# Joining a slot's score matmuls and V matmuls, and writing the mask with ScalarE, in a six-layer local-attention kernel

## The chip, the cores and the metric

The kernel runs on one core of a Trainium2 chip. The core has a matmul engine (TensorE, PE in the profile, with PEld for its weight loads), a vector engine (VectorE, DVE), an activation engine (ScalarE, ACT), a general engine (GpSimd, POOL) and a queue that issues DMAs (SyncE, SP). Each engine takes its own instructions in order; between engines they wait for semaphores. Matmul results go to PSUM, which has eight banks of 128 partitions by 512 fp32 numbers; everything else lives in SBUF. The metric is device time in microseconds; the profile is of one execution.

## The reference

The input `x` has shape (8, 512, 128): 8 sequences of 512 rows. Two residual blocks follow each other. The first is a layer norm, a linear recurrence with `tanh` over the 512 rows, and another layer norm. The second is a layer norm and six layers of local attention and a gated FFN:

```
def step(h, xb_t):
    h = jnp.tanh(h @ A.T + xb_t)
...
for i in range(DEPTH):
    x = attn_layer(shift_tokens(x), Wqkv[i], q_scale[i], k_scale[i], Wo[i]) + x
    x = ffn_layer(shift_tokens(x), ln_g[i], ln_b[i], W1[i], b1[i], W2[i], b2[i]) + x
```

Attention has 16 heads of 64. Queries and keys are normalised to length 1, scaled and rotated. A block of 32 queries sees 64 keys: its own 32 and the 32 before them. What lies outside the band of 32 back is masked, and so are the keys before the first row:

```
mask = (it < jb) | (it > jb + w) | (jb == -1)
sim = jnp.einsum('bhwie,bhwje->bhwij', bq, bk2) * QK_SCALE
sim = jnp.where(mask, -jnp.finfo(sim.dtype).max, sim)
attn = jax.nn.softmax(sim, -1)
out = jnp.einsum('bhwij,bhwje->bhwie', attn, bv2)
```

## The kernel before

The attention's work is cut into 96 groups, listed in `todo`. In layers 1 to 5 a group is one sequence and one half of the heads (8 heads: 4 pairs, `GP`). In layer 0, whose input comes out of the recurrence row by row, a group is 128 rows of four sequences and one half of the heads (`ChunkGroup`). A group is worked through in four slots, t = 0 to 3, of 128 queries each.

`slot(n, t)` writes out by hand, in program order, what the engines do in one slot. It works on several groups at once: the scores of group n at t (`cur`), the transposed probabilities and V products of the slot before (`last`, one slot late), the transposed outputs two slots late (`back`), the norms and values of group n+1 (`one`), and in slots 2 and 3 the query and key projections of group n+2 (`two`). Five lists `fill[0]` to `fill[4]` hold the work that stands between the pieces of attention; `run(k)` issues one of them. The engines take the instructions in this order.

The steps that the change and the prediction touch:

- `mask` (line 617): four bf16 matmuls of a 64x64 block of the identity with the mask array write the mask into two PSUM banks (`sc`, one per head of a pair) and open the accumulation.
- `scores` (line 634): small fp32 matmuls of 64 rows by 32 columns, which run beside each other in the array, add the scores. Each counts as two in the profile. A slot has 64 in the profile: 32 for pairs 0 and 1, 32 for pairs 2 and 3. The two halves are called apart, with `turn`, `turn_back` and `run(1)` between them.
- `less_max` (line 651): VectorE takes the maximum (L654) and subtracts it (L657); this frees the two banks.
- `exps` (line 663): ScalarE takes the exponential (L664). From group 9 on it stands before `run(2)`, in groups 0 to 8 behind it.
- `turn` (line 666): PE transposes the probabilities into `tp` (L670), ScalarE copies them out as `eT` (L675). `turn_back` (line 713) does the same for the outputs (`at` L718, `aoT` L722).
- `average` (line 677): the V products `av` (L689), again 32 and 32, in the two `acc` banks that `tp` and `at` had before. `divide` (line 699) is VectorE's reciprocal (L706) and product (L707), which frees those banks.
- `unit_a` and `unit_b` (lines 498, 512): projections `rawa` and `rawb` (L504, L516), ScalarE's squares (L508, L520) and scaled copy `bs` (L522), VectorE's `t` (L494), and GpSimd's two operations (L526, L527).
- `sums` (`nsq`, L533, copied as `ns`, L543), `norms` (`nt`, L415, then VectorE's solve, L427 to L437), `norms_back` (`kt`, L444, and ScalarE's copy `kn`, L451), `spread` (`bc`, L559), `finish` (VectorE's L567 and the DMAs of `qT` and `kbuf`), `values` (`vps`, L589, copied into `vbuf` by ScalarE, L598), `between` (DMAs inside `vbuf`), `project` (`yo`, L727) and `add` (L738).
- In the groups of layer 0 up to group 8 the recurrence runs inside the slots: `rec.tick(us)` (line 370) adds up the PE work issued, and issues one step (a matmul L295 and a `tanh` L303) when it reaches `PACE`, 0.35, and resets the sum. One call issues at most one step. `rec.need(c)` (line 377) issues what is missing of chunk c, steps and VectorE pieces, when a group needs it.
- `Feed` (line 816) is the FFN of four sequences. It takes part in the slots of 11 groups: in slot 0 `centre` stands in `fill[2]` and `fill[3]`, in slot 2 `apply` stands before `less_max`. The twelfth runs behind the last group.

PSUM is full: two banks for `sc`, two for `acc`, and four for all other products (`mm`; in the recurrence three and one for `xb`).

Of the kernel before, what the change touches and what calls it, by code (L numbers as in the profile page):

```python
# [7 lines left out]
F32 = mybir.dt.float32  # L8
# [6 lines left out]
B, S, D = 8, 512, 128  # L15
P = 128
DEPTH = 6
HEADS = 16
DH = 64
# [8 lines left out]
GP = 4  # L28
NG = NPAIR // GP

QB = 32
KB = QB + WINDOW
NT = S // P
# [15 lines left out]
def mk_seq_preln_kernel(  # L49
# [18 lines left out]
    nc = tc.nc  # L68
# [97 lines left out]
    with tc.tile_pool(name="qk", bufs=2) as qkp, tc.tile_pool(  # L166
        name="ao", bufs=1
    ) as aop, tc.tile_pool(name="tmp", bufs=2) as tmp, tc.tile_pool(
        name="e", bufs=1
    ) as ep, tc.tile_pool(name="small", bufs=4) as small, tc.tile_pool(  # L170
        name="rec", bufs=1
# [213 lines left out]
        rec = Recurrence()  # L385

        def shifted(b, buf):

            xs = xbufs[buf]
            nc.sync.dma_start(xs[: D // 2, WINDOW:], xT[: D // 2, b, :])  # L390
            nc.sync.dma_start(xs[D // 2 :, WINDOW + 1 :], xT[D // 2 :, b, : S - 1])
            return xs
# [61 lines left out]
        class Group:  # L454
# [161 lines left out]

            def mask(self, t):


                sct = scp.tile([P, 2, S], F32, tag="sc", name=f"sc_{self.nm}_{t}")  # L620
                self.sc = sct[:, :, : GP * KB].rearrange("p a (i k) -> p a i k", k=KB)
                for blk in range(2):
                    for par in range(2):
                        rows = slice(par * DH, (par + 1) * DH)
                        nc.tensor.matmul(
                            self.sc[blk * DH : (blk + 1) * DH, par],
                            ident_b[rows, rows],
                            mask_sb[rows, 0 if blk == 0 and self.first(t) else 1],
                            start=True,
                            stop=False,  # L630
                            skip_group_check=True,
                        )

            def scores(self, t, pairs):
                for i in pairs:
                    for blk in range(BT):
                        for par in range(2):
# [10 lines left out]
                            )  # L648
                rec.tick(0.4)

# [25 lines left out]

            def average(self, t, pairs):
                if pairs[0] == 0:
                    self.avs = [
                        accp.tile(  # L680
                            [P, GP, P], F32, tag="acc", name=f"av_{self.nm}_{t}_{par}"
                        )
                        for par in range(2)
                    ]
                for i in pairs:
                    for blk in range(BT):
                        for par, av in enumerate(self.avs):
# [8 lines left out]
                            )  # L696
                rec.tick(0.4)

# [296 lines left out]
        def slot(n, t, feed=None):  # L995
# [60 lines left out]
            if cur:  # L1056
                cur.mask(t)
                cur.scores(t, (0, 1))
            if last:
# [3 lines left out]
            run(1)  # L1063
            if cur:
                cur.scores(t, (2, 3))
            if feed and t == 2:
# [8 lines left out]
            if cur and n < NREC:  # L1075
                cur.exps()
            if last:
                last.average(lt, (0, 1))
            if one and t == 1:
                one.finish(1)  # L1080
                if not feed:
                    one.finish(2)
                    one.finish(3)
            run(3)
            if last:
                last.average(lt, (2, 3))
                last.divide(lt)
# [80 lines left out]
def _constants():  # L1168
# [4 lines left out]
    f = np.float32  # L1173
# [92 lines left out]
```

## Time and profile before

| | us |
|---|---|
| median of three runs | 4030.38 |
| lowest, highest | 4025.12, 4033.03 |
| span of the profiled execution | 4029.1 |
| PE busy | 3780.6 (94%) |
| DVE busy | 2496.4 (62%) |
| ACT busy | 1859.4 (46%) |
| POOL busy | 1824.5 (45%) |
| mask matmuls (L625, layers 1 to 5), busy | 97.1, 1280 matmuls |
| score matmuls (L641, layers 1 to 5), busy | 295.7, 20480 matmuls |
| V matmuls (L689, layers 1 to 5), busy | 307.6, 20480 matmuls |

The times agree within 0.2%, and the profiled execution lies 1.3 us under the median. Busy time is the time in which at least one instruction of the engine runs; matmuls are pipelined, so it is not time at PE's peak. In the profile's groups a row gives the line, the engine, the operation, output and inputs by the program's names, and then busy time, mean duration, and the idle time before it with what ended it. In a timeline a row begins with the start and the duration in microseconds; matmuls of one kind that follow each other stand in one row with their count, and a bracket holds the idle time of the engine just before and what ended it. The stride, from one row's start to the next one's on PE, tells what a piece costs, since PE's ends overlap.

### The profile page before, as it was taken

The page shows a single profiled execution, that of the slowest core. Times are in us where ns is not written, and L with a number is a line of the kernel's source. Part 1 is how long each engine was busy: PE and PEld are TensorE (multiplying, and loading weights), DVE is VectorE, ACT ScalarE, POOL GpSimd, SP SyncE. Part 2 cuts the span into 40 slices and gives each one's busy share as a digit, 9 for nine tenths or more (in the row PEclk, how much of TensorE's full clock was granted, in tenths as well). Part 3 has the DMA queues.
Part 4 walks back from the last instruction along what each step waited for, and adds up shares of the span by engine and source line. Part 5 has one row for each costly group of instructions (what it writes and reads, how often), then busy time and mean ns, then how long its engine had stood idle before and what let it go on. Part 6 is the DMA issues. An engine that isn't in the chain of part 4 may idle for free.

```text
span 4029.1 us, 147937 instructions
## 1 busy us (share of the span) xinstructions
PE 3780.6 (94%) x64726; PEld 1982.0 (49%) x64726; DVE 2496.4 (62%) x5209; ACT 1859.4 (46%) x3696; POOL 1824.5 (45%) x781
## 2 busy tenths in 40 slices
PE   5798997999999999999999999999999999999997
PEld 4555564444444444445444445454454444444453
DVE  3345646666576566566566566566566666676663
ACT  1243343445445455455455455455455445455442
POOL 0143323535355356366366366355355355355350
PEclk9888878999999999999999999999999999999998
DMA  3042343554344355344345345245344355354342
GB/s 108 23 109 64 87 96 75 117 128 93 84 110 110 72 116 117 83 111 111 73 107 127 79 102 119 65 112 129 74 104 113 69 123 120 75 113 106 74 108 61
DMA packets 366032, 389.51 MB, mean 97 GB/s; under 512 B 96974, under 2 KB 262348, under 8 KB 365260
## 3 DMA queue, kind: packets, MB, share of 16 engines
q1 hardware_dynamic: 364380, 378.09, 41.0%
q8 instruction: 512, 8.39, 0.9%
q10 hardware_dynamic: 1008, 1.96, 0.1%
q14 instruction: 132, 1.08, 0.1%
HBM read 34.25 MB, written 14.20 MB: 12 GB/s over the span
## 4 chain that ended last, share of the span: by engine, by line
PE 77%; DVE 13%; ACT 5%; issue 3%; DMA 1%; SPq 1%; ACTq 0%; DVEq 0%
PE vps L589 7%; PE yo L727 6%; PE rawb L516 6%; PE rawa L504 5%; PE sc L641 5%; PE tp L670 5%; PE xb L295 4%; PE av L689 4%; PE nsq L533 4%; PE at L718 4%; PE yf L948 3%; PE fa L922 3%; DVE t L567 3%; PE fg L926 3%; PE bc L559 2%
## 5 line engine op out<-in xcount | busy, mean ns | idle before, releaser
L526 POOL TENSOR_TENSOR u<-rope_sb,bs 128x1024 f32<-128x1024 f32 x320 | 766.4, 2395 | 1437.9 <-ACT bs L522 1311.1
L527 POOL TENSOR_TENSOR t<-t,u 128x1024 f32<-128x1024 f32 x320 | 755.7, 2362 | 25.1
L494 DVE SCALAR_TENSOR_TENSOR t<-rawa,par_sb,rope_sb 128x1024 f32<-128x1024 f32 x320 | 408.9, 1280 | 206.8 <-ACT sq L508 196.6
L664 ACT ACTIVATE e<-e 128x512 f32<-128x512 f32 x320 | 201.7, 630 | 609.6 <-DVE e L657 602.8
L567 DVE TENSOR_TENSOR t<-t,bc 128x1024 f32<-128x1024 f32 x320 | 376.5, 1215 | 159.0 <-PE bc L559 159.0
L689 PEld LDWEIGHTS av<-vbuf,eT 64*32 64x32 f32 x20480 | 208.4, 106 | 367.8 <-issue 254.0
L504 PE MATMUL rawa<-xbuf,wqk 128*128 128x512 f32 x640 | 357.7, 641 | 2.3 <-DMA xbuf<-xT 1.3
L589 PE MATMUL vps<-wv,xbuf 128*64 128x256 f32 x2560 | 346.7, 393 | 0.0
L516 PE MATMUL rawb<-xbuf,wqk 128*128 128x512 f32 x640 | 343.8, 619 | 0.0
L727 PE MATMUL yo<-aoT,wo 128*128 128x512 f32 x640 | 296.0, 605 | 41.4 <-DVE t L567 40.8
L641 PEld LDWEIGHTS sc<-kbuf,qT 64*32 64x32 f32 x20480 | 191.9, 106 | 245.2 <-issue 206.7
L689 PE MATMUL av<-vbuf,eT 64*32 64x65 f32 x20480 | 307.6, 224 | 3.0 <-issue 1.5
L508 ACT ACTIVATE sq<-rawa 128x512 f32<-128x512 f32 x320 | 188.3, 588 | 241.3 <-PE rawa L504 241.0
L295 PEld LDWEIGHTS xb<-hT,s1w 128*128 128x128 f32 x1022 | 202.8, 239 | 189.8 <-ACT hT L303 119.4
L641 PE MATMUL sc<-kbuf,qT 64*32 64x64 f32 x20480 | 295.7, 223 | 0.3 <-issue 0.3
L654 DVE TENSOR_REDUCE mx<-sc 128x8 f32<-128x512 f32 x320 | 220.0, 687 | 110.0 <-PE sc L641 110.0
L707 DVE TENSOR_TENSOR ao<-av,rc 128x256 f32<-128x256 f32 x640 | 271.8, 425 | 22.0
L675 ACT COPY eT<-tp 128x512 f32<-128x512 f32 x320 | 189.0, 591 | 188.2 <-PE tp L670 188.2
L295 PE MATMUL xb<-hT,s1w 128*128 128x8 f32 x1022 | 223.7, 292 | 44.1 <-ACT hT L303 43.3
L303 ACT ACTIVATE hT<-xb 128x8 f32<-128x8 f32 x512 | 91.0, 178 | 355.3 <-PE xb L295 338.0
L657 DVE TENSOR_TENSOR e<-sc,mx 128x512 f32<-128x512 f32 x320 | 221.3, 692 | 17.7 <-DVE mx L654 0.9
L670 PE MATMUL tp<-ident,e 128*128 128x128 f32 x1280 | 208.4, 285 | 18.6 <-DVE rc L706 15.8
(321 smaller groups left out, 6093.2 us busy)
## 6 DMA issues: line engine op xcount, KB each, us to landing
qT<-t SPq DMA_DIRECT2D x640, 128.0 KB
kbuf<-t SPq DMA_DIRECT2D x640, 128.0 KB
vbuf<-vbuf SPq DMA_DIRECT2D x544, 130.0 KB
vbuf<-vbuf SPq DMA_DIRECT2D x160, 97.5 KB
xbuf<-xT SPq DMA_DIRECT2D x95, 128.0 KB
xbuf<-xT SPq DMA_DIRECT2D x80, 127.8 KB
wqk<-in_w_qkv SPq DMA_DIRECT2D x12, 512.0 KB
xf<-xT SPq DMA_DIRECT2D x24, 256.0 KB
```

The lines of the kernel that those rows point to most:

```text
L295: nc.tensor.matmul(self.xb[:, k, :], abc[:, 0, :], self.hT[:, (t - 1) % P, :], start=False, stop=True, skip_group_check=True,)
L494: nc.vector.scalar_tensor_tensor(t, self.twice(raw), scale, self.rope(isk, 1), ALU.mult, ALU.mult)
L504: nc.tensor.matmul(raw, self.wqk[:, c, 0], self.xs[:, WINDOW:], start=True, stop=True)
L516: nc.tensor.matmul(raw, self.wqk[:, c, 1], self.xs[:, WINDOW:], start=True, stop=True)
L526: nc.gpsimd.tensor_mul(self.wide(u), self.rope(isk, 0), self.twice(bs))
L527: nc.gpsimd.tensor_add(self.ts[c], self.ts[c], u)
L567: nc.vector.tensor_mul(t, t, self.bcs[c].unsqueeze(1).to_broadcast([P, 2, S]))
L589: nc.tensor.matmul(ps[par * KB : (par + 1) * KB, j], self.xs[:, k0 : k0 + KB], self.wv[:, par * GP * DH : (par + 1) * GP * DH], start=True ...
L641: nc.tensor.matmul(self.sc[blk * QB : (blk + 1) * QB, par, i, :], self.qT[rows, i, q0 : q0 + QB], kT[rows, i, :], start=False, stop=True, ...
L670: nc.tensor.transpose(tp[:, i, :], self.e[:, i].rearrange("p a k -> p (a k)"), ident)
L689: nc.tensor.matmul(av[blk * QB : (blk + 1) * QB, i, :VW], self.eT[rows, i, blk * QB : (blk + 1) * QB], self.v[rows, BT * t + blk, i, :], s ...
L727: nc.tensor.matmul(self.yp, wo[:, self.g * GP + c, :], self.aoT[:, c, :], start=(c == 0), stop=(c == GP - 1),)
```

## The change

The two score banks are allocated once, at the start, and two matmuls write them once so that later matmuls add to what stands there. In a slot, `mask(t)` is now one ScalarE copy of the mask array into both banks, repeated over the two heads of a pair. It is issued one slot ahead, behind the exponential and `run(2)`: slot t writes the mask for slot t + 1, and slot 3 that for slot 0 of the next group. The 64 score matmuls of a slot stand together at the place of the first half, and the 64 V matmuls together at the place of their first half, between `run(2)` and `run(3)`. Each calls `rec.tick` once, with 0.8, where there were two calls with 0.4. `one.finish(1)` keeps its place ahead of the V matmuls, `finish(2)` and `finish(3)` come behind them. The mask array on the host has 128 rows by block in place of 64 rows twice.

```diff
         rec = Recurrence()
...

+        sct = scp.tile([P, 2, S], F32, tag="sc", name="sc")
+        for par in range(2):
+            nc.tensor.matmul(
+                sct[:, par, : GP * KB],
+                ident_b,
+                mask_sb[:, 0].rearrange("p i k -> p (i k)"),
+                start=True,
+                stop=True,
+                skip_group_check=True,
+            )
+        sc = sct[:, :, : GP * KB].rearrange("p a (i k) -> p a i k", k=KB)
...
             def mask(self, t):
-                sct = scp.tile([P, 2, S], F32, tag="sc", name=f"sc_{self.nm}_{t}")
-                self.sc = sct[:, :, : GP * KB].rearrange("p a (i k) -> p a i k", k=KB)
-                for blk in range(2):
-                    for par in range(2):
-                        rows = slice(par * DH, (par + 1) * DH)
-                        nc.tensor.matmul(
-                            self.sc[blk * DH : (blk + 1) * DH, par],
-                            ident_b[rows, rows],
-                            mask_sb[rows, 0 if blk == 0 and self.first(t) else 1],
-                            start=True,
-                            stop=False,
-                            skip_group_check=True,
-                        )
-
-            def scores(self, t, pairs):
-                for i in pairs:
+                m = mask_sb[:, 0 if self.first(t) else 1]
+                nc.scalar.copy(sc, m.unsqueeze(1).to_broadcast([P, 2, GP, KB]))
+
+            def scores(self, t):
+                self.sc = sc
+                for i in range(GP):
...
-                rec.tick(0.4)
+                rec.tick(0.8)
...
-            def average(self, t, pairs):
-                if pairs[0] == 0:
-                    self.avs = [
...
-                for i in pairs:
+            def average(self, t):
+                self.avs = [
...
+                for i in range(GP):
...
-                rec.tick(0.4)
+                rec.tick(0.8)
...
             run(0)
             if cur:
-                cur.mask(t)
-                cur.scores(t, (0, 1))
+                cur.scores(t)
             if last:
                 last.turn(lt)
             if back:
                 back.turn_back(bt)
             run(1)
-            if cur:
-                cur.scores(t, (2, 3))
             if feed and t == 2:
                 feed.apply()
...
             run(2)
             if cur and n < NREC:
                 cur.exps()
-            if last:
-                last.average(lt, (0, 1))
+            if cur and t + 1 < NT:
+                cur.mask(t + 1)
+            elif one and t == NT - 1:
+                one.mask(0)
             if one and t == 1:
                 one.finish(1)
-                if not feed:
-                    one.finish(2)
-                    one.finish(3)
+            if last:
+                last.average(lt)
+            if one and t == 1 and not feed:
+                one.finish(2)
+                one.finish(3)
             run(3)
             if last:
-                last.average(lt, (2, 3))
                 last.divide(lt)
...
-    r = np.arange(2 * QB)[:, None]
+    r = np.arange(P)[:, None]
...
-    mask = np.tile(np.stack([first, band], 1), (2, 1, 1))
+    mask = np.stack([first, band], 1)
```

More of the change, by code (lines that the diff above doesn't have):

```diff
@@ L675, in turn @@
                 nc.scalar.copy(self.eT, tp)
-            def average(self, t, pairs):
-                if pairs[0] == 0:
-                    self.avs = [
[L680 to L684, printed above, removed]
-                for i in pairs:
+            def average(self, t):
+                self.avs = [
+                    accp.tile(
+                        [P, GP, P], F32, tag="acc", name=f"av_{self.nm}_{t}_{par}"
+                    )
+                    for par in range(2)
+                ]
+                for i in range(GP):
                     for blk in range(BT):
```

## The prediction

> **What bounds the kernel now.** I read the page first (busy shares, chain, groups), then the timeline of one ordinary group of four slots, then the stretches by slot. On the page TensorE is the engine that is nearly always busy, and the chain that ended last runs mostly through it; VectorE holds 13% of that chain, ScalarE 5%.
>
> ```profile
> span 4029.1 us, 147937 instructions
> PE 3780.6 (94%) x64726; PEld 1982.0 (49%) x64726; DVE 2496.4 (62%) x5209; ACT 1859.4 (46%) x3696; POOL 1824.5 (45%) x781
> PE 77%; DVE 13%; ACT 5%; issue 3%; DMA 1%; SPq 1%; ACTq 0%; DVEq 0%
> ```
>
> By slot (slots 0, 1, 2, 3 of one group, cut at its mask matmuls) the columns are length, then busy time of PE, PEld, DVE, ACT, POOL, then the granted clock. Slots 0, 2 and 3 leave PE next to no idle time, slot 1 leaves 0.6 us.
>
> ```profile
> 2022.44:2029.35 6.91, 6.91 (x176) 4.50 (x172) 4.09 (x15) 2.66 (x5) 6.75 (x4) 1.00 0.31 71
> 2029.35:2038.65 9.30, 8.72 (x159) 4.31 (x159) 6.99 (x11) 3.27 (x7) 0.34 (x1) 1.00 0.64 145
> 2038.65:2045.48 6.83, 6.83 (x149) 3.31 (x148) 4.98 (x8) 5.03 (x9) 2.89 (x2) 1.00 0.78 173
> 2045.48:2054.49 9.01, 8.80 (x173) 3.90 (x172) 6.12 (x13) 5.62 (x10) 8.93 (x4) 1.00 0.08 18
> ```
>
> A busy PE does not mean that PE sets the pace. The timeline from the end of slot 0 into slot 1 shows a chain over three engines: DVE subtracts the maximum (L657, late, since the solve of the norms stands before it), ACT takes the exponential, two V copies and `kn`, PE spreads (`bc`), DVE multiplies (L567), and only then `yo` starts, after 0.57 us of idle PE.
>
> ```profile
> 2028.15 0.69 DVE L657 TENSOR_TENSOR e<-sc,mx 128x512 f32<-128x512 f32 x1
> 2028.94 0.63 ACT L664 ACTIVATE e<-e 128x512 f32<-128x512 f32 x1 [2.68 <-DVE e L657]
> 2029.35 0.30 PE L625 MATMUL sc<-mask_sb,ident_b 64*64 64x256 bf16 x4
> 2029.47 1.05 ACT L598 COPY vbuf<-vps 128x512 f32<-128x512 f32 x2
> 2030.42 0.60 ACT L451 COPY kn<-kt 128x512 f32<-128x512 f32 x1
> 2031.07 1.14 PE L559 MATMUL bc<-kn,selt_sb 32*128 32x512 f32 x8
> 2033.57 3.70 PE L727 MATMUL yo<-aoT,wo 128*128 128x512 f32 x8 [0.57 <-DVE t L567]
> ```
>
> In slots 2 and 3 the pace is a loop of DVE and ACT: maximum and subtraction, exponential, square, `t`, division, and PE's `tp` of slot 3, which waits for the division. Its one hole is 0.54 us before the maximum, for the second half of the scores.
>
> ```profile
> 2041.74 0.69 DVE L654 TENSOR_REDUCE mx<-sc 128x8 f32<-128x512 f32 x1 [0.54 <-PE sc L641]
> 2044.40 1.28 DVE L494 SCALAR_TENSOR_TENSOR t<-rawa,par_sb,rope_sb 128x1024 f32<-128x1024 f32 x1 [1.24 <-ACT sq L508]
> 2046.38 0.63 PE L670 MATMUL tp<-ident,e 128*128 128x128 f32 x4 [0.20 <-DVE rc L706]
> ```
>
> **The change, part by part.** I take it around an ordinary group, 32.05 us from 2022.44 to 2054.49, by strides (start to start). There are 96 groups: the first 9 hold the recurrence, 11 an FFN inside, the last 2 lack successors; 74 are ordinary.
>
> Joining. A half of 32 score or V matmuls takes 0.38 to 0.41. A joined group of 64, called S, is not in the trace, but 62 V matmuls behind a wait are, beside 32 that are alone: 0.85 against 0.46, so 30 more cost 0.39.
>
> ```profile
> 3944.22 0.46 PE L689 MATMUL av<-vbuf,eT 64*32 64x65 f32 x32
> 3947.48 0.85 PE L689 MATMUL av<-vbuf,eT 64*32 64x65 f32 x62 [0.25 <-ACT aoT L722]
> ```
>
> Hence S = 0.38 + 0.39 = 0.77: nothing gained inside the group. Bounds: 0.65 (0.27 from L641 to the L689 that follows it directly, plus 0.38) and 0.86 (0.27 plus the 0.59 that this L689 shows). What is gained lies at the neighbours. In the FFN group a `raw` pair takes 0.97 (2277.92 to 2278.89) between a small and a large group, 0.85 between two large ones, 0.96 before the mask; between two small ones it takes 1.06 (2042.98 to 2044.04).
>
> ```profile
> 2277.92 1.12 PE L504 MATMUL rawa<-xbuf,wqk 128*128 128x512 f32 x2
> 2278.89 1.02 PE L516 MATMUL rawb<-xbuf,wqk 128*128 128x512 f32 x2
> 2279.74 1.02 PE L504 MATMUL rawa<-xbuf,wqk 128*128 128x512 f32 x2
> ```
>
> The mask. PE loses four matmuls a slot, 0.23. ACT gets one 128x512 copy into two banks; no row has ACT writing PSUM. Copies of that shape out of PSUM take 0.59 to 0.61 and follow each other at 0.48, the slowest ACT row of that shape 0.69. I take M = 0.60 for the copy's own length, between 0.48 and 0.69.
> The Trainium skill ("ScalarE: Activation LUTs", Step-by-step: what each stage is for) says that ScalarE reaches PSUM sooner than SBUF; by that M would lie lower, perhaps 0.55 as an estimate, and the sum 4 us lower; no row here shows it.
>
> Now the path. (A) Slot 0, its start to the end of L657: mask 0.23 and half 0.41 become S with its DMA waits, 0.80; `tp` 0.49, `at` 0.44, then the norms on DVE as before: +0.16.
> (B) End of L657 (2028.84) to `bc`: before 2.23. The copy for slot 1 stands on ACT behind the exponential and a V copy, and slot 1's scores wait for it; behind them on PE wait `tp`, `at` and `bc`. After: wait 0.10, exponential 0.53, V copy 0.48, M 0.60, semaphore 0.06, S 0.77, `tp` 0.49, `at` 0.53 = 3.56, so +1.33. `kn`, 0.48 later on ACT, is ready by then. PE, through with `kt`, stands idle for about 1.7 us; its mask matmuls had been cover for just this time.
> (C) `bc` to the maximum of slot 2: 10.67 before. All DVE from `t` on; the 0.54 hole goes, since the scores are complete, and DVE overlaps 0.09 more: -0.63. The V half behind `yo` (0.39) leaves PE here, off the path, which is DVE's.
> (D) Maximum to `tp` of slot 3: 4.64, unchanged; ACT's copy stands behind the square, and slot 3's scores have 0.7 us of slack before `tp`.
> (E) `tp` of slot 3 to the end of `nsq`: before 8.11 (2046.38 to 2054.49). After: 0.54, 0.47, `rawb` 0.86, `rawa` 0.96, S 0.77, `rawb` 0.97, V 1.02, `nsq` 1.85 = 7.44, so -0.67.
> Sum: +0.16 + 1.33 - 0.63 - 0.67 = +0.19 us a group, as 3 S + M - 2.72; times 74 is +14.
>
> FFN groups: ACT is on the path in slot 0 (eight centring steps, copy among them, with the +0.16: +0.64), then S for 0.61 (+0.16), -0.2 in slot 2 at the removed half, -0.3 behind the FFN, -0.5 in slot 3: -0.2 each, 11 of them: -2, give or take 6.
>
> Recurrence (to 704 us). `tick(0.4)` twice becomes `tick(0.8)` once, so each slot issues two steps fewer. In the new order 15 of 512 steps run alone, 4 before chunk 1 and 11 before chunk 3, at 0.86 (the spacing of L303 at 35 us) in place of about 0.25 inside slots ((8.70 - 6.83)/10 and (12.21 - 9.01)/13): +9. Two chunk outputs then start their DVE normalisation later: about +5, bounds -5 and +15. The mask and joins give 0.4 in some 35 slots, -14; ACT's copy before tanh, at most 0.48 in 32 slots, half of it taken: +8, with 0 and 15 as bounds. Together +8, from -24 to +25; I take +3, as PE is full there and shorter slots also bring the pieces earlier.
>
> At nothing: two matmuls that write the banks at the start (PE is idle then for 29 us); the mask array's new rows (same size); DMAs (none moves past another, and the V moves on SP follow the first V copy, ahead of the mask copy); POOL, which waits 1311 us for `bs` and has room for 0.5.
>
> Total: 4029.1 + 14 - 2 + 3 = 4044. The profiled span lies 1.3 under the median of the runs, 4030.4: forecast 4045.
>
> **The rivals.**
> 1. Faster: the joined group streams at the lower bound. S = 0.65 makes a group 0.17 us shorter: -13 - 2 + 3 = 4018. It decides from S below 0.71. For it: L641 followed by L689 strides only 0.27. Against: the 62 row.
> 2. Much slower: the clock. Behind the new wait of (B), a stretch of 3.4 us holds little but `kt`, 64 scores and `tp`. After 1.28 us of idle PE late in the run the clock was 0.50 for 6.8 us:
>
> ```profile
> 3922.90:3926.30 3.40, 1.95 (x132) 1.34 (x126) 2.41 (x6) 1.25 (x3) 0.00 (x0) 1.00 0.63 140
> 3926.30:3933.10 6.80, 6.24 (x134) 4.23 (x142) 2.41 (x6) 2.27 (x4) 0.00 (x0) 0.50 0.44 99
> 3953.60:3957.00 3.40, 2.03 (x72) 1.39 (x70) 0.97 (x5) 1.07 (x2) 0.00 (x0) 1.00 0.00 0
> ```
>
> The last row speaks against it: as little work, and the clock stayed; my stretch has 1.7 busy of 3.4. If it falls, `tp`, `at` and `bc` at half speed cost 1.7 us on the path, in perhaps 40% of 74 groups (the share of starts for which the stretch is that thin): +50, 4095.
> The Trainium skill ("TensorE: Matmul & The Clock Gate", HAM oscillation) asks only that no gap exceed some 3.4 us; by it 1.7 us would be harmless and the sum stay 4045. The rows above differ: 1.28 us was followed by the half clock, and the rival stands by them.
> 3. It cancels: within 8 us, 4030. S and M need only be 0.04 smaller each.
>
> **How the numbers follow.** Slower by the sum 0.44, the clock 0.14, cancelled 0.17, faster 0.25. A difference under 0.2% (8 us) can't be told from none. Hence slower 0.58, same 0.17, faster 0.25. With S from 0.65 to 0.86 and M from 0.48 to 0.69 the ordinary groups give -22 to +41, the recurrence 15 either way; with the clock at the top: 4010 to 4096.
>
> **What would show it.** Right: slot 1's scores waiting for ACT's copy, 1.2 to 2 us; no wait for scores before the maximum in slot 2; `raw` pairs of 0.85 to 0.97; a group of 32.2. Wrong: no wait in slot 1 (then (B) is 0.48, `kn` alone being later, the group 31.4, all 3981); S outside 0.65 to 0.86; a clock under 1 between 704 and 3926 us.

## The result

The changed kernel takes 4031.31 us in the median of 20 runs (4022.87 to 4037.77), the kernel before 4021.16 in the median of 20 (4011.41 to 4033.03): a ratio of 1.0021, with a 95% interval of 1.0012 to 1.0030, so 8 us slower, 5 to 12. The three runs shown ahead of the prediction lay high among the 20 of the kernel before. The profiled execution of the changed kernel has a span of 4025.5 us and a time of 4027.33; it lies 4 us below its median, and the one of before 9 us above its own. The two profiles taken alone therefore say that the change gained 3.6 us; a difference of this size is read from the medians.

From the page of the changed kernel: the span, TensorE's busy time, the chain, and the group of the score matmuls (busy time and mean ns of one, then the idle time before them and what ended it).

```profile
span 4025.5 us, 145489 instructions
PE 3635.0 (90%) x63192; PEld 2039.5 (51%) x63192; DVE 2462.1 (61%) x5209; ACT 2046.7 (51%) x4080; POOL 1823.4 (45%) x781
PE 54%; DVE 18%; ACT 6%; issue 2%; DMA 1%; SPq 0%; ACTq 0%; DVEq 0%
L641 PE MATMUL sc<-kbuf,qT 64*32 64x64 f32 x20480 | 280.2, 224 | 115.7 <-ACT sc L631 114.2
```

TensorE is busy 146 us less, and ScalarE 187 us more. Against that stands one new wait of 114 us: the scores wait for ScalarE's mask copy. The slots of one ordinary group of the changed kernel, cut where the scores begin (columns as in the prediction: length, then busy time of PE, PEld, DVE, ACT, POOL, the granted clock, DMA):

```profile
2002.38:2010.68 8.30, 6.67 (x173) 4.72 (x169) 4.78 (x17) 3.89 (x8) 8.01 (x4) 1.00 0.26 60
2010.68:2019.48 8.80, 8.23 (x154) 4.38 (x154) 5.73 (x6) 3.14 (x6) 0.00 (x0) 1.00 0.61 138
2019.48:2025.88 6.40, 6.38 (x145) 3.56 (x144) 4.98 (x10) 4.75 (x9) 2.20 (x1) 1.00 0.78 174
2025.88:2034.70 8.82, 8.40 (x167) 4.08 (x166) 6.41 (x13) 6.75 (x13) 8.66 (x5) 1.00 0.18 40
```

The cuts are not at the same place of the work as before (there the mask matmuls began a slot), so the wait, which stands ahead of slot 1's scores, is counted in the first row: 1.63 us of idle PE. The wait itself, in the timeline of the changed kernel (start, duration, engine, line; L641 scores, L631 mask copy, L610 V copies, L463 `kn`, L571 `bc`):

```profile
2008.25 0.69 DVE L657 TENSOR_TENSOR e<-sc,mx 128x512 f32<-128x512 f32 x1
2009.03 0.63 ACT L664 ACTIVATE e<-e 128x512 f32<-128x512 f32 x1 [2.61 <-DVE rc L705]
2009.57 0.57 ACT L610 COPY vbuf<-vps 128x512 f32<-128x512 f32 x1
2010.03 0.59 ACT L631 CAST sc<-mask_sb 128x512 f32<-128x512 bf16 x1
2010.68 0.86 PE L641 MATMUL sc<-kbuf,qT 64*32 64x64 f32 x64 [1.64 <-ACT sc L631]
2011.03 0.60 ACT L463 COPY kn<-kt 128x512 f32<-128x512 f32 x1
2011.47 0.66 PE L670 MATMUL tp<-ident,e 128*128 128x128 f32 x4
2012.49 1.14 PE L571 MATMUL bc<-kn,selt_sb 32*128 32x512 f32 x8
```

The copy stands behind the exponential and one V copy, as the prediction's step (B) has it; `kn` is ready at 2011.63, 0.86 us before `bc` starts. In slot 2 the maximum no longer waits for scores, and slot 3's `tp` waits for the division as before:

```profile
2022.46 0.68 DVE L654 TENSOR_REDUCE mx<-sc 128x8 f32<-128x512 f32 x1
2027.16 0.63 PE L670 MATMUL tp<-ident,e 128*128 128x128 f32 x4 [0.42 <-DVE rc L705]
```

By stretches of the two profiles: group 9 begins at 723.8 us before and at 699.0 after (-24.8); from there to group 94 it takes 3181.3 and 3199.8 (+18.5); from group 94 to the end 124.0 and 126.8 (+2.8). So the groups without the recurrence lose, and the stretch with it gains. How much of the -24.8 belongs to the change and how much to the single execution is what the first experiment asks.

### The profile page after: what moved, and what is told of

It is laid out like the page before. It is cut to its first block, busy times and chain, and to the rows that moved or that the text cites. A ratio compares the mean times of both kernels' runs of the same rounds, so it can differ in the third digit from the quotient of the medians.

```text
span 4025.5 us, 145489 instructions
## 1 busy us (share of the span) xinstructions
PE 3635.0 (90%) x63192; PEld 2039.5 (51%) x63192; DVE 2462.1 (61%) x5209; ACT 2046.7 (51%) x4080; POOL 1823.4 (45%) x781
## 4 chain that ended last, share of the span: by engine, by line
PE 54%; DVE 18%; ACT 6%; issue 2%; DMA 1%; SPq 0%; ACTq 0%; DVEq 0%
PE yo L726 6%; PE sc L641 6%; PE rawb L528 5%; PE rawa L516 5%; PE tp L670 5%; PE at L717 4%; PE nsq L545 4%; DVE t L579 3%; PE yf L947 3%; PE fa L921 3%; PE fg L925 3%; DVE t L506 3%; DVE e L657 3%; PE bc L571 2%; PE vps L601 2%
## 5 line engine op out<-in xcount | busy, mean ns | idle before, releaser
L641 PEld LDWEIGHTS sc<-kbuf,qT 64*32 64x32 f32 x20480 | 226.7, 105 | 323.5 <-ACT sc L631 178.2
L641 PE MATMUL sc<-kbuf,qT 64*32 64x64 f32 x20480 | 280.2, 224 | 115.7 <-ACT sc L631 114.2
L688 PEld LDWEIGHTS av<-vbuf,eT 64*32 64x32 f32 x20480 | 227.1, 105 | 223.8 <-ACT sq L532 110.7
L601 PE MATMUL vps<-wv,xbuf 128*64 128x256 f32 x2560 | 330.3, 389 | 2.7 <-ACT xf L848 2.7
L516 PE MATMUL rawa<-xbuf,wqk 128*128 128x512 f32 x640 | 328.3, 594 | 1.7 <-DVE t L506 1.7
L688 PE MATMUL av<-vbuf,eT 64*32 64x65 f32 x20480 | 281.6, 225 | 5.7 <-issue 2.3
L657 DVE TENSOR_TENSOR e<-sc,mx 128x512 f32<-128x512 f32 x320 | 221.4, 692 | 22.0 <-PE rawa L516 0.5
L601 PEld LDWEIGHTS vps<-wv,xbuf 128*64 128x64 f32 x2560 | 161.5, 136 | 144.8 <-issue 62.0
```

Of the source, the lines that this page charges most:

```text
L516: nc.tensor.matmul(raw, self.wqk[:, c, 0], self.xs[:, WINDOW:], start=True, stop=True)
L601: nc.tensor.matmul(ps[par * KB : (par + 1) * KB, j], self.xs[:, k0 : k0 + KB], self.wv[:, par * GP * DH : (par + 1) * GP * DH], start=True ...
L641: nc.tensor.matmul(self.sc[blk * QB : (blk + 1) * QB, par, i, :], self.qT[rows, i, q0 : q0 + QB], kT[rows, i, :], start=False, stop=True, ...
L688: nc.tensor.matmul(av[blk * QB : (blk + 1) * QB, i, :VW], self.eT[rows, i, blk * QB : (blk + 1) * QB], self.v[rows, BT * t + blk, i, :], s ...
```

## The experiments

Most of the kernels below are one file with settings for the groups 0 to 8 (`REC`) and for the later ones (`REST`): the mask on ScalarE at the place of the change (`act`), ahead of the exponential in slot 0 (`first`), or on TensorE as before (`pe`); scores joined (`js`), V products joined (`jv`); and, for halves, the two step calls (`tk`). A joined group calls once, with 0.8. In groups that are set as before, the file's bank for the scores is still the one allocated at the start; an ordinary group so set takes 32.04 us in the seven kernels that change groups 0 to 8 alone, 32.05 in the kernel before.

```diff
+            how = REC if n < NREC else REST
...
             if cur:
-                cur.scores(t)
+                if how["mask"] == "pe":
+                    cur.pe_mask(t)
+                if how["js"]:
+                    cur.scores(t, allp, 0.8)
+                else:
+                    cur.scores(t, lo, how["tk"][0])
...
             run(1)
+            if cur and not how["js"]:
+                cur.scores(t, hi, how["tk"][1])
```

For the ordinary groups the tables use the prediction's steps, as medians over the 69 of them from group 15 on: (A) slot 0 to the end of L657, (B) to `bc`, (C) to the maximum of slot 2, (D) to `tp` of slot 3, (E) to the end of the group.

### Where the time goes: recurrence or later groups (rec_new)

```diff
+        REC = {'mask': 'act', 'js': 1, 'jv': 1, 'tk': (0.4, 0.4)}
+        REST = {'mask': 'pe', 'js': 0, 'jv': 0, 'tk': (0.4, 0.4)}
```

> Groups 0 to 8 (those with the recurrence) as in the changed kernel, all later groups as before. Theory of the forecast: the recurrence stretch gains nothing (+3 us, from -24 to +25), so the kernel takes +3 us against before, ratio about 1.001. Theory from the profile of the changed kernel: in it group 9 began at 699.0 against 723.8 us, while the later groups lost 18.5 and the end 2.8; the recurrence stretch is then where the change gains, and as the medians differ by +10, the gain is 10 - 18.5 - 2.8 = -11 us, ratio 0.997; the other 14 of the 25 are differences between single executions. Groups from 10 on at 32.04, no scores waiting for ScalarE.

Measured: 4001.93 us, ratio 0.9966 (0.9954 to 0.9979), -14 us. The change makes the recurrence stretch faster, and the forecast for it, +3 us, is wrong. By subtraction the rest of the change costs 1.0021 - 0.9966, 22 us; the two profiles gave 18.5 + 2.8 = 21.3.

### Fewer steps in a slot (rec_ticks)

```diff
+        REC = {'mask': 'pe', 'js': 0, 'jv': 0, 'tk': (0.8, 0)}
+        REST = {'mask': 'pe', 'js': 0, 'jv': 0, 'tk': (0.4, 0.4)}
```

> The kernel before, but the first half of the scores and of the V products calls the recurrence with 0.8 and the second half not at all: one step in place of two at each, everything else as before. Theory of the forecast: fewer steps in the slots, more of them alone before a chunk is needed, and two chunk outputs later: +9 + 5 = +14 us, slots 0 and 2 of groups 2 to 7 shorter by 0.5. Rival: the steps are what makes the slots long, and fewer of them in a slot explain the gain of the recurrence stretch: -10 us or more.

Measured: 4025.14 us, ratio 1.0013 (1.0001 to 1.0025), +5 us. Most of the slots 0 and 2 are shorter by 0.58 and 0.44 us, as expected, and more steps run behind the slots: the last one at 659 us, in the profile of before at 625. The sign of the forecast's term was right, its size (+14) too large. The gain of -14 does not come from here.

### The two halves of the change in the ordinary groups (joins_pe, first0)

joins_pe is the changed kernel with the mask back on TensorE; first0 is the changed kernel with slot 0's copy ahead of the exponential.

```diff
+        REC = {'mask': 'pe', 'js': 1, 'jv': 1, 'tk': (0.4, 0.4)}
+        REST = {'mask': 'pe', 'js': 1, 'jv': 1, 'tk': (0.4, 0.4)}
```

> The changed kernel with the joined scores and V products in their new places, but with the mask written by four TensorE matmuls ahead of the scores of the same slot, as before. Theory A (the steps of the forecast, with S = 0.79 and without the copy): an ordinary group changes by +0.39 (slot 0 to the end of L657), +0.32 (from there to bc), -0.63 (bc to the maximum of slot 2), -0.44 (tp of slot 3 to nsq) = -0.36, so 31.68 us; times 74 is -27 us, and no clock falls between 710 and 3900 us; with the recurrence between -11 and +5 and FFN groups at -2: -40 to -24 us, ratio 0.990 to 0.994. Rival B: the joined groups cost something that the steps leave out, and the mask on ScalarE is not what costs: the group stays at 32.2 or more, ratio 1.00.

```diff
+        REC = {'mask': 'act', 'js': 1, 'jv': 1, 'tk': (0.4, 0.4)}
+        REST = {'mask': 'first', 'js': 1, 'jv': 1, 'tk': (0.4, 0.4)}
```

> The changed kernel, but in slot 0 of the groups from 9 on ScalarE's mask copy stands ahead of the exponential and the V copy, in the other slots where the change put it. Theory A (the wait in slot 1 is ScalarE's queue ahead of the copy): the copy starts when L657 ends, slot 1's scores wait some 0.6 us in place of 1.64, bc is then held by kn, whose ScalarE queue is as long as in the changed kernel: about 2.7 us behind the end of L657 in place of 3.55, a group of 31.5, no fall of the clock in slot 1; -0.8 x 74 = -60 us against the changed kernel, -50 against before, ratio 0.987. Rival B: what holds slot 1 is the copy's own path into the banks or kn, and the order on ScalarE matters little: a group of 32.0 or more, ratio 0.999 to 1.002 against before.

| | A | B | C | D | E | group | ratio to before |
|---|---|---|---|---|---|---|---|
| before | 6.40 | 2.22 | 10.67 | 4.64 | 8.11 | 32.05 | 1 |
| changed | 6.52 | 3.55 | 9.97 | 4.70 | 7.54 | 32.29 | 1.0021 (1.0012 to 1.0030) |
| joins_pe | 6.76 | 2.22 | 10.04 | 4.70 | 7.54 | 31.27 | 0.9860 (0.9845 to 0.9876) |
| first0 | 6.53 | 2.68 | 10.04 | 4.70 | 7.54 | 31.50 | 0.9875 (0.9857 to 0.9893) |

The joins alone make a group 0.78 us shorter: 1.20 is gained in (C) and (E), and (A) and (D) give 0.42 of it back. With the joins in place, the copy behind the exponential and a V copy costs 1.02: 1.33 in (B), less 0.24 in (A), where the mask's matmuls stood, and 0.07 in (C). Theory A for joins_pe was too small by half, in two places: (B) does not grow, since `kn` sets `bc` there and the longer scores end just ahead of it, and (E) holds no mask that could be taken out or put back. The timeline of joins_pe:

```profile
2018.63 0.30 PE L637 MATMUL sc<-mask_sb,ident_b 64*64 64x256 bf16 x4
2018.86 0.86 PE L654 MATMUL sc<-kbuf,qT 64*32 64x64 f32 x64
2020.14 0.60 PE L733 MATMUL at<-ident,ao 128*128 128x128 f32 x4
2020.15 0.60 ACT L463 COPY kn<-kt 128x512 f32<-128x512 f32 x1
2020.80 1.14 PE L571 MATMUL bc<-kn,selt_sb 32*128 32x512 f32 x8
```

The mask and the scores start 0.05 us after L657 ends (2018.58), where they waited 1.74 in the changed kernel. TensorE's four mask matmuls cost nothing in slot 1: it would be idle for `kn` otherwise. In first0 the copy starts when L657 ends, and everything behind it shifts by about what was expected (31.5 and -50 us):

```profile
2017.68 0.69 DVE L671 TENSOR_TENSOR e<-sc,mx 128x512 f32<-128x512 f32 x1
2018.41 0.59 ACT L631 CAST sc<-mask_sb 128x512 f32<-128x512 bf16 x1 [2.55 <-DVE e L671]
2019.05 0.86 PE L654 MATMUL sc<-kbuf,qT 64*32 64x64 f32 x64 [0.56 <-ACT sc L631]
2020.41 0.60 ACT L463 COPY kn<-kt 128x512 f32<-128x512 f32 x1
2021.05 1.14 PE L571 MATMUL bc<-kn,selt_sb 32*128 32x512 f32 x8
```

So the cost is the copy's place in ScalarE's queue. `kn` now sets `bc`, at 2.68.

### The copy without the joins, and one join alone (act_split, joins_s)

```diff
+        REC = {'mask': 'pe', 'js': 0, 'jv': 0, 'tk': (0.4, 0.4)}
+        REST = {'mask': 'act', 'js': 0, 'jv': 0, 'tk': (0.4, 0.4)}
```

> From group 9 on ScalarE copies the mask, at the place of the change, but scores and V products stay in halves; groups 0 to 8 as before. Theory A (the copy's place behind the exponential and a V copy is the cost, whatever is joined): slot 0 to the end of L657 -0.23, from there to bc 0.10 + 0.53 + 0.48 + 0.60 + 0.06 + 0.38 + 0.49 + 0.53 = 3.17 in place of 2.22, +0.95, the rest between 0 and -0.2: +0.5 to +0.7 a group, 74 x that = +37 to +52 us, ratio 1.009 to 1.013. Rival B (the wait costs only because 64 scores stand behind it): +0.2 a group or less, ratio below 1.004.

Measured: 4047.45 us, ratio 1.0060 (1.0039 to 1.0082); the group is 32.43, +0.38: (A) -0.30, (B) 3.15, +0.93, (C) -0.24. The sum is between the two theories, but (B) is what theory A said, with halves too. The copy thus costs 0.38 a group beside halves and 1.02 beside joins; its price depends on the other part.

```diff
+        REC = {'mask': 'pe', 'js': 0, 'jv': 0, 'tk': (0.4, 0.4)}
+        REST = {'mask': 'pe', 'js': 1, 'jv': 0, 'tk': (0.4, 0.4)}
```

> Only the scores joined, from group 9 on; mask on TensorE, V halves and groups 0 to 8 as before. Theory A (the scores carry the gain of the joined group: the hole before the maximum of slot 2 goes): slot 0 to the end of L657 +0.36, to bc 0 (kn holds it, as in joins_pe), to the maximum of slot 2 -0.6, slot 3 -0.3: -0.5 a group of the -0.78 of joins_pe, -38 us, ratio 0.990. Rival B (the V products carry it: joined, they leave the neighbours of DVE's division and nsq free): 0 to -0.2 a group, -15 us or less, ratio 0.996 or more.

Measured: 3999.81 us, ratio 0.9937 (0.9918 to 0.9957); group 31.69, -0.36, with (A) +0.35, (C) -0.63, (D) +0.58, (E) -0.66. The scores alone close the hole ahead of the maximum, but slot 3's `tp` comes later; joining the V products as well takes (D) back to 4.70. The result lies between the two theories: the joined scores bring 0.36 of the 0.78, and the V products on top of them the other 0.42. The V products joined alone were not run in these groups.

### The copies of slots 1 to 3 (double_123)

```diff
                 cur.mask(t + 1)
+                if n >= NREC and t > 0:
+                    cur.mask(t + 1)
             elif one and t == NT - 1:
                 one.mask(0)
+                if n >= NREC:
+                    one.mask(0)
```

> The changed kernel, but behind slots 1, 2 and 3 of the groups from 9 on the mask copy is made twice. Theory A (the forecast's zeros: the copies of these slots lie beside other work): 0 to +0.1 a group, 0 to +8 us against the changed kernel, ratio 1.002 to 1.004 against before. Rival B (ScalarE's squares in slots 2 and 3 stand behind the copy, and DVE's t and the norms of slot 3 wait for them): +0.48 for one or two of the copies, +36 to +71 us, ratio 1.011 to 1.020.

Measured: 4026.01 us, ratio 1.0019 (1.0005 to 1.0032), the same as the changed kernel. That is the sum of two differences that the traces show: an ordinary group is 0.12 shorter (32.17 in the median, with (B) 3.49 and (D) 4.64), and the groups with an FFN are 1.04 longer each (73.61 against 72.57 in the mean of ten). In slot 2 of an ordinary group the doubled copy, 1.21 us, makes the scores of slot 3 wait, and nothing behind them is later:

```profile
2027.68 1.21 ACT L631 CAST sc<-mask_sb 128x512 f32<-128x512 bf16 x2
2028.95 0.95 PE L641 MATMUL sc<-kbuf,qT 64*32 64x64 f32 x64 [0.29 <-ACT sc L631]
```

The forecast's zeros for the copies of three slots hold in the ordinary groups: there only slot 0's copy is on the path. In the groups with an FFN a second copy is not free. Why an ordinary group is a little shorter with it is open.

### What gains in the recurrence stretch (rec_joins, rec_act, rec_js, rec_jv, rec_tv)

`REST` is as before in all of them. In `REC`, rec_joins has both joins with the mask on TensorE, rec_act the copy with halves, rec_js and rec_jv one join each, rec_tv halves with one step call in place of two at the V products alone.

```diff
+        REC = {'mask': 'pe', 'js': 1, 'jv': 1, 'tk': (0.4, 0.4)}
```

> Groups 0 to 8 with the joined scores and V products and one step call each, but with the mask on TensorE; later groups as before. Measured so far: the whole change in these groups -14 us, one step call in place of two +5. Theory C (clock): with joined pieces the stretch spends some 125 us of half clock in place of some 160 (profiles of the changed kernel, of joins_pe and first0 against before and rec_ticks), worth up to half of 35 = 17 us where TensorE is full, and 0.1 to 0.2 a slot; so about +5 - 17 - 3 = -15 us, ratio 0.996. Theory M (mask): the gain comes from the mask's matmuls leaving TensorE, and this kernel stands where rec_ticks stands, 0 to +5 us, ratio 1.000 to 1.001.

```diff
+        REC = {'mask': 'act', 'js': 0, 'jv': 0, 'tk': (0.4, 0.4)}
```

> Groups 0 to 8 with the mask copied by ScalarE, halves apart and two step calls each as before; later groups as before. Forecast: -0.23 of TensorE in 36 slots, -8, and the copy ahead of tanh, +8: 0 us. Theory C (clock): half-clock time as before, about 160 us, so 0 to -5 us. Theory M: with the joins at 0 the copy carries the whole of -19 us, ratio 0.995.

```diff
+        REC = {'mask': 'pe', 'js': 1, 'jv': 0, 'tk': (0.4, 0.4)}
```

> Groups 0 to 8 with only the scores joined (one step call for them), the rest as before. rec_joins took -15 us, and its profile has 85 us of TensorE work at half clock before group 9, against 104 to 125 in the four profiles with halves, each of which has one stretch of 20 to 58 us at half clock that the joined ones lack. Theory A: each join does part, -5 to -10 us and a shorter long stretch. Rival B: the joined scores alone end the long stretch, -12 us or more. Rival C: the scores do nothing here, 0 to +5.

```diff
+        REC = {'mask': 'pe', 'js': 0, 'jv': 1, 'tk': (0.4, 0.4)}
```

> Groups 0 to 8 with only the V products joined (one step call for them), the rest as before. Theory A: -5 to -10 us. Rival B: the joined V products alone end the long stretch at half clock, -12 us or more. Rival C: 0 to +5.

```diff
+        REC = {'mask': 'pe', 'js': 0, 'jv': 0, 'tk': (0.4, 0.4), 'tv': (0.8, 0)}
...
-                    last.average(lt, lo, how["tk"][0])
+                    last.average(lt, lo, how["tv"][0])
...
-                    last.average(lt, hi, how["tk"][1])
+                    last.average(lt, hi, how["tv"][1])
```

> The kernel before, with halves everywhere, but in groups 0 to 8 the V products call the recurrence once with 0.8 (in the first half) and the scores twice as before: the step calls of rec_jv without its join. Theory A (joining the V products is what gains, by less time at half clock): 0 to +5 us, ratio 1.000 to 1.001, TensorE work at half clock above 100 us as in before and rec_ticks. Theory B (the number of steps in a slot sets the gain of rec_jv): -20 us or more, ratio 0.995 or less.

From the granted clock and TensorE's busy time in each profile: the time at half clock, in stretches that begin between 200 and 705 us, the TensorE work in it, the start of group 9's first maximum, and that start less half of the work at half clock (an estimate of what full clock would have saved). Beside them stand the timed ratio and the same in us, and from all timed runs the mean granted clock less that of the kernel before (in thousandths), and what it makes of the time by the estimate below.

| REC | half clock | PE work in it | group 9 | less half | ratio to before | us | clock of the runs | us by it |
|---|---|---|---|---|---|---|---|---|
| before | 160 | 125 | 729 | 666 | 1 | 0 | 0 | 0 |
| rec_act | 157 | 123 | 735 | 673 | 1.0026 (1.0013 to 1.0040) | +10 | -2.4 | +8 |
| rec_ticks | 164 | 118 | 729 | 671 | 1.0013 (1.0001 to 1.0025) | +5 | -2.0 | +6 |
| rec_js | 130 | 87 | 712 | 669 | 0.9980 (0.9968 to 0.9992) | -8 | +1.2 | -4 |
| rec_new | 130 | 83 | 705 | 664 | 0.9966 (0.9954 to 0.9979) | -14 | +1.7 | -5 |
| rec_joins | 133 | 85 | 707 | 665 | 0.9962 (0.9949 to 0.9976) | -15 | +1.9 | -6 |
| rec_tv | 106 | 65 | 701 | 669 | 0.9959 (0.9943 to 0.9975) | -16 | +3.2 | -10 |
| rec_jv | 113 | 76 | 700 | 661 | 0.9931 (0.9911 to 0.9951) | -28 | +4.7 | -15 |

Group 9's start is spread over 35 us; less half of the work at half clock the spread is 12. In these profiles, then, what most of the kernels differ in is how long TensorE works at half clock.

The timed runs show the same, less strongly. The clock moves from run to run with the code unchanged: in the 92 runs of the kernel before that were taken beside these experiments it lies between 0.971 and 0.979, and within each set the time follows it (correlation -0.97), by 3.2 us for each 0.001. Taken at that price, as an estimate, the kernels' mean clocks give the last column. The spread of 38 us shrinks to 15, from +2 (rec_act) to -13 (rec_jv), but of rec_new's -14 the clock makes only 5.

One profile says little about a long stretch. act_split and joins_s have groups 0 to 8 as before, and their profiles have 108 and 104 us of work at half clock where before has 125 (group 9 at 724 and 720, less half 670 and 668). The change's order stands in these groups of the changed kernel, first0, best2 and double_123 too, with 79 to 83 us (702 to 707, less half 662 to 665), as in rec_new. So the difference in work at half clock is more than the spread between executions, some 30 us in place of 42, and half of it is 15; the rest of the stretch is then about 5 us shorter. Between these 15 us and the 5 of the timed runs the clock's share stays open.

One stretch of the kernel before shows it (each row 20 us; PE's busy time stands behind the length, the granted clock is the third number from the end):

```profile
500.00:520.00 20.00, 20.00 (x204) 12.64 (x204) 9.95 (x29) 5.72 (x21) 0.00 (x0) 0.50 0.41 102
520.00:540.00 20.00, 19.69 (x153) 11.66 (x146) 12.29 (x37) 4.03 (x15) 0.00 (x0) 0.50 0.28 61
```

and the same stretch of rec_tv:

```profile
500.00:520.00 20.00, 16.29 (x253) 10.20 (x252) 13.65 (x31) 7.50 (x25) 8.28 (x4) 0.84 0.39 81
520.00:540.00 20.00, 16.65 (x214) 10.63 (x215) 12.69 (x31) 9.00 (x28) 10.64 (x5) 0.80 0.10 22
```

In the first TensorE is idle for 0.31 of 40 us, and the clock stays at 0.50 all the same. In act_split, whose groups 0 to 8 are as before, the same 40 us have a clock of 0.80 and 0.83, and no half-clock stretch in its profile is longer than 31 us; in joins_s, again as before there, one lasts 58. The long stretch thus comes and goes without any change of the order.

Of the expectations, rec_joins fell as theory C said (-15), so the mask's matmuls are not the gain; with the copy besides, rec_new takes no more (-14), and the copy with halves costs 10, which none of its three theories had. The joins alone, against rec_ticks, are worth 20 us. rec_js met theory A and rec_jv rival B, but the reason given there, that the join itself ends the long stretch, is not upheld: rec_tv has no join at all and takes -16, with the least work at half clock in these eight profiles (over all timed runs rec_jv has the higher clock), where its theory A said 0 to +5. Its theory B said -20 or more. So the one step call at the V products gives some 16 of rec_jv's 28 and its join the other 12, while the same call at both places (rec_ticks) costs 5. The pieces do not add up. That the clock makes part of each difference is argued, from the profiles and from the runs of one kernel that differ in clock; no experiment sets the clock. Why one order of steps and small matmuls has more work at half clock than another is open.

### An earlier bc, and the parts put together (best2, best3)

best2 is joins_pe, with the recurrence of the changed kernel, and two pieces moved in slots 0 and 1:

```diff
+                fill[2] = [lambda: one.values(1, True)]
+                fill[3] = [lambda: one.values(2, True)]
...
+                    fill[0] += [
+                        lambda: one.keep_values(1),
+                        lambda: one.keep_values(2),
+                        lambda: one.between(0),
+                    ]
...
+            if early and t == 1:
+                run(1)
             if last:
                 last.turn(lt)
```

> Groups 0 to 8 as in the changed kernel; later groups as joins_pe (mask on TensorE, all joined), and besides, in groups without an FFN, ScalarE copies kn ahead of two V copies, and bc stands between the scores and tp of slot 1. Theory A (in joins_pe kn sets bc, 2.22 us behind the end of L657): exponential 0.53, kn 0.60 and 0.1 for semaphores bring bc to about 1.3, so 0.9 a group less if DVE's chain from t on keeps its 10.04: 74 x -0.9 = -67 us against joins_pe, about 3885 us, ratio 0.968. Rival B: the V copies, now behind kn, hold bc's banks or the aoT copy, and yo and the projections come later: 0 to -25 against joins_pe, ratio 0.980 to 0.986.

Measured: 4017.20 us, ratio 0.9981 (0.9970 to 0.9992), 49 us behind joins_pe. (B) fell to 1.25 as planned, but (C) rose to 11.10 and (D) to 5.55. The timeline of best2 (L617 V copies, L710 V products):

```profile
2014.07 2.10 PE L571 MATMUL bc<-kn,selt_sb 32*128 32x512 f32 x8
2014.56 0.29 PEld L571 LDWEIGHTS bc<-kn,selt_sb 32*128 32x128 f32 x2 [0.19 <-ACT vbuf L617]
2017.48 0.30 PE L710 MATMUL av<-vbuf,eT 64*32 64x65 f32 x2 [0.29 <-ACT eT L696]
2017.97 0.68 PEld L710 LDWEIGHTS av<-vbuf,eT 64*32 64x32 f32 x62 [0.35 <-ACT aoT L744]
```

`bc`, 1.14 long elsewhere, takes 2.10, since its later banks are those of the V copies that now stand behind `kn`; then the V products wait for ScalarE's `eT` and `aoT`, and `yo` and slot 2's projections come late. It is rival B, and stronger: a queue that is relieved at its head has its own tail to pay.

best3 joins only the V products in groups 0 to 8, and both afterwards, with the mask on TensorE everywhere:

```diff
+        REC = {'mask': 'pe', 'js': 0, 'jv': 1, 'tk': (0.4, 0.4)}
+        REST = {'mask': 'pe', 'js': 1, 'jv': 1, 'tk': (0.4, 0.4)}
```

> Mask on TensorE everywhere; groups 0 to 8 with only the V products joined, as rec_jv; later groups with scores and V products joined, as joins_pe. If the two parts add up: joins_pe 0.986 with -28 in place of -15 us in the first groups, about 3946 us, ratio 0.982 to 0.984. Rival (the gain of rec_jv over rec_joins is spread between chips and runs): 0.986 as joins_pe.

Measured: 3943.56 us (3940.08 to 3949.46), ratio 0.9816 (0.9792 to 0.9839). The two parts add up; it is the fastest of all, by its ratio 74 us ahead of the kernel before. From its page:

```profile
span 3938.3 us, 148147 instructions
```

## Why the prediction was right or wrong

**Sign and size.** Forecast were +15 us against the 4030.4 of before; measured +8 (5 to 12). Slower was the likeliest case, and it is slower, but by little more than half of what was forecast, and that is the sum of two errors: +22 in the later groups where the forecast had +12, and -14 in the recurrence stretch where it had +3.

**S and M.** 64 scores take 0.79 (2010.68 to 2011.47), 0.77 was taken: joining saves nothing inside the group. The copy is 0.59 long and the scores start 0.65 after it does, 0.66 was taken. The Trainium skill's sentence on ScalarE and PSUM ("ScalarE: Activation LUTs", Step-by-step: what each stage is for) would have made it shorter; the run shows 0.59, as long as the copies into SBUF beside it (0.57 to 0.60).

**The steps of an ordinary group.** (A) +0.16 forecast, +0.12 measured; (B) +1.33 and +1.33; (C) -0.63 and -0.70; (D) 0 and +0.06; (E) -0.67 and -0.57; the sum +0.19 and +0.24. The mechanism was right in each: the new wait of 1.64, the copy's place behind the exponential and a V copy (first0, act_split), the copies of the other slots at nothing (double_123, in ordinary groups). Over the 69 groups it makes +16.4 us, the three falls of the clock included.

**FFN groups.** -0.2 each was forecast; they go from 72.38 to 72.57 in the mean of ten, +0.2. The term was mis-sized by 4 us. The forecast let the copy cost 0.64 in slot 0 and the other steps gain 0.84; in the traces the joins without the copy make such a group 0.45 longer (joins_pe, 72.83), and the copy without the joins 0.39 shorter (act_split, 71.99). In which slots is not shown.

**The clock behind the new wait (rival 2).** The price was right and the frequency was not: 1.7 us in 40% of 74 groups were forecast, and it is 1.6 us (33.9 against 32.3) in 3 groups of the profiled execution, 5 us in all. A clock under 1 between 704 and 3926 us was among the forecast's signs of being wrong, and here it is; in before's profile no such fall lies between 704 and 3900 us. The three windows around the first, cut at the clock's own steps:

```profile
2574.44:2577.85 3.41, 1.78 (x72) 1.35 (x71) 1.68 (x5) 2.60 (x5) 3.33 (x3) 1.00 0.05 13
2577.85:2581.26 3.41, 3.41 (x16) 1.67 (x14) 0.00 (x0) 1.17 (x2) 1.92 (x1) 0.50 0.74 173
2581.26:2584.68 3.42, 2.84 (x73) 1.64 (x70) 3.14 (x4) 0.53 (x1) 0.00 (x0) 1.00 0.42 95
```

The first holds 1.78 us of TensorE work in 3.41, as the forecast had it (1.7 of 3.4); `tp`, `at` and `bc` behind it run at half clock. Of 43 such windows (at most 53% busy) in the later groups, 40 kept the clock and 3 lost it. The rule of the Trainium skill ("TensorE: Matmul & The Clock Gate", HAM oscillation), that only a gap over some 3.4 us matters, would have none of them: the idle time is 1.64. The measurement decides: such a gap is not harmless, and it is nearly so. The prediction's own row from the end of the kernel before is less direct than it was read: the idle 1.28 us run from 3925.58 to 3926.86, and the clock fell at 3926.3, before they were over; what it shares with the three falls is the thin window ahead, 1.95 us of work in 3.40.

**The recurrence stretch.** This is the step that failed: "+9", "about +5", "-14", "+8", together +8, of which +3 was taken. Fewer steps in a slot, 9 + 5 = 14 in the forecast, cost 5 (rec_ticks). Of the -14 for mask and joins, 0.23 in 36 slots are the mask's, -8, and -6 the joins'; against rec_ticks the joins took -20 (rec_joins). The mask's leaving and the copy ahead of `tanh`, -8 and +8, come to about +1 beside the joins (rec_new against rec_joins), as forecast, though to +10 with halves (rec_act). So 5 - 20 + 1 stands where 14 - 6 + 0 was forecast: the steps cost less, and the joins gained three times as much. What the sum had no term for is the clock: TensorE works less at half clock after the change (79 to 83 us in five profiles, against 104 to 125 in three). Priced by the clocks of the timed runs, as an estimate, 12 of the joins' 20 us are the clock, which leaves 8, near the 6 of the forecast, and the steps cost nothing beyond it. How much of the whole -14 is the clock, 5 us by the timed runs or up to 15 by the profiles, stays open. The lower bound of the term, -24, does not come out of the bounds given for its parts either: 9 - 5 - 14 + 0 is -10, and the measured -14 lies below that. The profile of before showed the low clock, with a granted clock of 0.83 between 200 and 690 us, and the prediction asked of the clock only in the later groups, where it stood at 1.00.

**Rivals 1 and 3.** S is not 0.65, and no gain came from it; the kernel isn't faster. A cancelled change (within 8 us) comes close in size, but by the recurrence stretch and not by a smaller S or M.

**The range.** 4010 to 4096 holds 4031. That owes something to luck, since a miss of 10 us upwards in the later groups and of 17 downwards in the recurrence stretch offset each other. By the bounds given with it, -22 in the ordinary groups where the sum has +14, and 15 less in the recurrence, the low end would have been 4045 - 36 - 15 = 3994. The chances for slower and within 0.2% were 0.58 and 0.17; the measured 0.21% lies at the bound between them.

## What to carry to other kernels

A change with two parts is priced part by part: here the joins alone took off 56 us (0.9860; 15 of them in groups 0 to 8) and the mask on ScalarE, with the joins in place, cost 65 (1.0021 against 0.9860), though it took work off the engine that was busy for 94% of the time; in slot 1 TensorE's mask matmuls stood where it had to wait anyway. Work that is moved to an engine with room must be followed through that engine's queue, to the one place where somebody waits for it, and it belongs at the head of that queue, not behind the work of others. Where a stretch runs with a granted clock below 1, a change of order in it can be worth some microseconds by the clock besides its own work, and a sum of durations taken at one clock does not find that.

## What the runs showed of the hardware

- TensorE stayed at half clock for 51 us while it was busy for 47 of them (489 to 540 us of before, where fp32 projections, small matmuls and recurrence steps of 8 columns alternate). With the same order in these groups, the longest such stretch was 58 us in joins_s and 31 in act_split.
- The granted clock varied between runs of one kernel (0.971 to 0.979 in 92 runs of before), and a run with 0.001 less took about 3.2 us longer.
- One step call less a slot took 16 us (rec_tv), two less cost 5 (rec_ticks): the prices of the pieces don't add up in this stretch.
- A second copy of 0.6 us in three of four slots made no ordinary group longer (32.17 us against 32.29) and each group with an FFN 1 us longer; one such copy in the fourth slot cost 1 us in each ordinary group.
